# Edge terms of four graphs: one product on a block-diagonal operand, or four short products on row groups

## The chip, the cores and the metric

The kernel runs on one core of a Trainium2 chip. The metric is the time of the program on the device, in microseconds, as the median of several runs. All data are fp32.

## The reference, cut to what matters

There are 128 graphs of 128 nodes with 256 channels each. The program is two graph layers, one after the other. The change lies in the first, in the branch that weighs messages by the distance of node features. With `h` the normalised input after a relu:

```
s    = h @ w_se.T + b_se                                  # 3 numbers for each node
sq   = sum(s * s, -1)
dist = sq[:, :, None] + sq[:, None, :] - 2 * s @ s.T      # for each graph, 128 x 128
A    = exp(-dist) * adj
msg  = relu(h @ w_msg.T + b_msg)
x_nmp = A @ msg                                           # for each graph
```

`x_nmp`, together with the output of a convolution branch (`x_conv`) and `h`, goes into a gated unit (three gates, 768 by 512 and 768 by 256 weights). The second layer runs five small graph convolutions on the first 25 nodes of each graph.

The exponent can be had from one matrix product with five rows for each graph. The left operand has the rows `2 s` (three), `-1` and `-sq`; the right one `s` (three), `sq` and `1`. Their product is `2 s s' - sq' - sq`, which is `-dist`.

## The kernel before

**Blocks.** Four graphs make a block (`BB` = 4), so there are 32 blocks. The program has a front part (normalisation, and the convolution through spectra), and then a loop over the 32 blocks that computes gates and, beside them, everything else that is left. Instructions of each engine run in a fixed order. In the loop that order is made by a scheduler of the framework from the program's order and from when it expects buffers and inputs to be ready; the front part has an order written by hand.

**The loop.** `gates(i, step, nxt)` computes the gated unit of block `i`. Its products (L599) are a Strassen scheme: 7 products of quarters for each gate part, each of up to three input pairs. After each of the 7 outputs, `between()` (here `step`) advances a generator by one step: either `beside_gates(i + 1)`, which makes the next block's inputs, or a piece of the second layer. `beside_gates` runs, in this order and spread over the steps, `messages` (L505 to L518), `conv_out` (L487 to L494), `edge_terms` (L525 to L529), `edges` (L538 to L541), `x_nmp` (L551 to L556) and the pieces of `back`, the end of block `i - 1`.

**Edge terms.** `messages` leaves the five-row operands in `lr`, in which the nodes stand on the partitions and each graph has a stretch of 32 columns, five of them filled (three sums, and the constants of L447 and L448). `edge_terms` transposes both halves of `lr` on TensorE (L525), so that graph `b` has its five rows on the partitions 32b to 32b+4. The left half is copied to `lt` by ScalarE (L527). The right half is copied by VectorE to `rt` (L529), four times side by side, and each copy is multiplied by a mask `bm`, which keeps only the 32 partitions of its own graph: `rt` is block-diagonal, 128 rows by 512 columns. `bm` is made once by GpSimd (L471 to L474). `edges` then needs one product of all 128 rows by 512 columns (L538) into one PSUM bank, one exponential over 512 columns on ScalarE (L540) and one product with the adjacency mask `at` on VectorE (L541). `x_nmp` takes the result `e` as the moving operand of eight products (L551).

**Banks.** All TensorE outputs are tiles of one pool with eight buffers, `bank()`, each one PSUM bank of 512 columns. A product that is given a bank waits until its last user has emptied it.

**Row groups.** One other place in the kernel has products on groups of 32 rows. `weight_spectra` (L162) keeps 17 taps on the partitions 32r to 32r+16 and issues four products in a row, for r from 0 to 3, each to a bank of its own.

**Names that the prediction uses.** `xc` (L494) is the convolution branch's output, made on ScalarE from `u` (L493, VectorE). `m` (L602, L610) is a gate output copied out of PSUM by ScalarE; `u` of L607, L612 and L617 and the outputs of L604, L614 and L620 are sums of gate outputs on VectorE and GpSimd. L633 works on the reset gate on VectorE. `ab` (L775, L780) and `hn` (L765, L766) are in `back`, and `xa` is where `ab` is stored by the queue of SyncE (SP). L575 makes operands of the Strassen scheme. `nt` and `dck` are small loads of the second layer.

Of the kernel before, what the change touches and what calls it, by code (L numbers as in the profile page):

```python
# [8 lines left out]
F32 = mybir.dt.float32  # L9
AF = mybir.ActivationFunctionType  # L10
ALU = mybir.AluOpType
AX = mybir.AxisListType

P = 128
# [3 lines left out]
BB = 4  # L18
# [56 lines left out]
def gnn_kernel(ctx: ExitStack, tc: tile.TileContext, io, out0: bass.AP, out1: bass.AP):  # L75
    nc = tc.nc
    x, adjT = io["x"], io["adjT"]
    B, N, D = x.shape
# [7 lines left out]
    cst = ctx.enter_context(tc.tile_pool(name="cst", bufs=1))  # L86
# [5 lines left out]
    def bank():  # L92
        return psum.tile([P, 512], F32, tag="bank", name="bank")
# [327 lines left out]
    wk = ctx.enter_context(tc.tile_pool(name="wk", bufs=1, reuse_waits="tile"))  # L421
# [5 lines left out]
    def load(i):  # L427
# [9 lines left out]
        for b in range(BB):  # L437
# [28 lines left out]
    nc.vector.tensor_mul(nb2, vec[:, V_B2:V_B2 + 5 * C].rearrange("p (g c) -> p g c", c=C),  # L466
                         nw[:, :, None].to_broadcast([P, 5, C]))


    bm = cst.tile([P, BB], F32)  # L470
    nc.gpsimd.memset(bm, 1.0)  # L471
    nc.gpsimd.affine_select(out=bm, in_=bm, compare_op=ALU.is_ge, fill=0.0, base=0,
                            pattern=[[-32, BB]], channel_multiplier=1)
    nc.gpsimd.affine_select(out=bm, in_=bm, compare_op=ALU.is_ge, fill=0.0, base=31,  # L474
                            pattern=[[32, BB]], channel_multiplier=-1)

    A_s, xcs, xns, ts, msgs, outs, lrs, xts = ({} for _ in range(8))

    def conv_out(i):
# [41 lines left out]
    def edge_terms(i):  # L521

        ps = bank()
        for k in range(2):
            nc.tensor.transpose(ps[:, k * P:(k + 1) * P], lr[:, k].rearrange("p b r -> p (b r)"), ident)  # L525
        lt = wk.tile([P, P], F32, tag="lt", name="lt", bufs=2)
        nc.scalar.copy(lt, ps[:, :P])  # L527
        rt = wk.tile([P, BB, N], F32, tag="rt", name="rt", bufs=1)
        nc.vector.tensor_tensor(rt, ps[:, None, P:2 * P].to_broadcast([P, BB, N]),  # L529
                                bm[:, :, None].to_broadcast([P, BB, N]), op=ALU.mult)  # L530
        lrs[i] = lt, rt

    def edges(i):

        at, _, _ = loaded.pop(i)
        lt, rt = lrs.pop(i)
        pd = bank()
        nc.tensor.matmul(pd, lt, rt.rearrange("p b n -> p (b n)"), start=True, stop=True)  # L538
        e = wk.tile([P, BB, N], F32, tag="e", name="e", bufs=1)
        nc.scalar.activation(e.rearrange("p b n -> p (b n)"), pd, AF.Exp)  # L540
        nc.vector.tensor_mul(e, e, at)  # L541
        A_s[i] = e

    def x_nmp(i):
# [391 lines left out]
    def beside_gates(i):  # L936

        ends = back(i - 2, *back_loads(i - 2)) if i > 1 else iter(())
        if i < NBLK:
            parts = messages(i)  # L940
            next(parts)
            yield
            next(parts)
            next(ends, None)
            yield
            inverse = conv_out(i)
            next(inverse)
            next(ends, None)
            yield
            edge_terms(i)  # L950
            next(ends, None)
            yield
            for _ in inverse:
                yield
            edges(i)
            yield
            next(ends, None)
            yield
            yield
            yield from x_nmp(i)  # L960
        for _ in ends:
            yield
            if i == NBLK:
                yield
# [174 lines left out]
```

## Time and profile before

| | |
|---|---|
| three runs | 1934.36, 1942.66, 1935.14 us; median 1935.14 |
| profiled execution, its own time | 1944.77 us |
| its span, first to last instruction | 1943.0 us |
| granted TensorE clock, mean | 0.992 of full speed |
| TensorE busy (matmuls) | 1901.1 us |
| VectorE, ScalarE, GpSimd busy | 1296.3, 713.2, 609.2 us |
| L538, both passes of 32 products | 64 records |
| moved from and to HBM | 178.66 and 85.14 MB |

How to read it: the profile is of one execution, whose own time is longer than the median of the three runs. PE is TensorE's matmuls, PEld its weight loads, DVE VectorE, ACT ScalarE, POOL GpSimd, SP SyncE, which only issues transfers here. An fp32 product appears as two records, one for each pass, so counts of matmuls are twice those of the program. The length of a matmul's record includes the way through the pipeline, and its end is modelled; what a matmul costs in a dense row is the distance to the start of the next. In the lines of groups, `out<-in` are the program's names, then come shapes, the count, and after the bar busy time, mean ns of one, and the idle time of the engine before them.

### The profile page before, as it was taken

Reading aid. Unit: us, or ns where it says so; the run is one execution under the profiler, and the core shown is the slowest. Engines: PE = TensorE matmul, PEld = TensorE weight load, DVE = VectorE, ACT = ScalarE, POOL = GpSimd, SP = SyncE. Lnnn points to the kernel's source line nnn. Section 1 sums busy time; section 2 is a strip of 40 time slices with the busy share of each in tenths; the row PEclk is TensorE's granted clock in tenths of the full one; section 3 lists DMA queues with packets and bytes.
Section 4 is the critical chain, followed back from the end, with each engine's and each line's share of the span. In section 5 each row is a group of like instructions: output and inputs, shape, how many; then the busy total and the mean of one; then the engine's idle time right before and its main releaser. Section 6 shows DMA issues by size and latency. Waiting matters only on the chain.

```text
span 1943.0 us, 29921 instructions
## 1 busy us (share of the span) xinstructions
PE 1901.1 (98%) x10418; PEld 1652.7 (85%) x10418; DVE 1296.3 (67%) x3247; ACT 713.2 (37%) x1459; POOL 609.2 (31%) x681
## 2 busy tenths in 40 slices
PE   8999898999899999999999999999999999999999
PEld 7888787988788888888888888888878888888887
DVE  5676457754587777777756577787756587777643
ACT  4553113421143334334333434334334434333334
POOL 1012442135233433443322243343322143343300
PEclk9999999999899999999999999999999999999999
DMA  8787975459843223233323533224333523222125
GB/s 309 293 315 226 323 260 194 142 181 309 267 135 98 72 72 102 68 81 110 81 84 92 142 81 100 70 71 116 86 82 87 147 75 105 74 72 64 44 88 154
DMA packets 248853, 265.76 MB, mean 137 GB/s; under 512 B 106850, under 2 KB 223927, under 8 KB 244223
## 3 DMA queue, kind: packets, MB, share of 16 engines
q1 hardware_dynamic: 236767, 196.74, 35.8%
q10 hardware_dynamic: 11936, 67.11, 8.9%
q8 instruction: 83, 1.36, 0.3%
q14 instruction: 67, 0.55, 0.1%
HBM read 178.66 MB, written 85.14 MB: 136 GB/s over the span
## 4 chain that ended last, share of the span: by engine, by line
PE 90%; DMA 6%; DVE 2%; issue 1%; ACT 1%; POOL 0%; SPq 0%; ACTq 0%; POOLq 0%; DVEq 0%
PE bank L599 44%; PE bank L314 6%; PE bank L505 5%; PE bank L919 5%; PE bank L859 5%; PE bank L223 5%; PE bank L487 3%; PE bank L551 3%; PE bank L238 3%; DMA v<-vd 3%; PE bank L309 3%; PE bank L490 1%; PE bank L162 1%; PE bank L538 1%; PE bank L838 1%; PE bank L770 1%
## 5 line engine op out<-in xcount | busy, mean ns | idle before, releaser
L599 PE MATMUL bank<-t,sw 128*128 128x256 f32 x1152 | 290.9, 379 | 0.2 <-POOL t L573 0.2
L612 POOL TENSOR_TENSOR u<-u,m 128x256 f32<-128x256 f32 x128 | 92.9, 726 | 594.4 <-ACT m L610 532.2
L599 PEld LDWEIGHTS bank<-t,sw 128*128 128x128 f32 x1152 | 215.3, 190 | 30.1 <-issue 2.3
L599 PE MATMUL bank<-t,wih 128*128 128x256 f32 x768 | 197.2, 379 | 0.0
L599 PEld LDWEIGHTS bank<-t,wih 128*128 128x128 f32 x768 | 143.4, 190 | 19.3 <-DVE u L617 0.5
L306 POOL TENSOR_TENSOR vs<-v 128x512 f32<-128x512 f32 x78 | 100.5, 1307 | 138.7 <-DMA v<-vd 74.9
L223 PE MATMUL bank<-wc,ht 128*128 128x256 f32 x512 | 125.1, 399 | 6.1 <-ACT ht L210 6.1
L505 PE MATMUL bank<-wms,ht 128*128 128x259 f32 x512 | 122.3, 381 | 0.0
L223 PEld LDWEIGHTS bank<-wc,ht 128*128 128x128 f32 x512 | 100.4, 201 | 22.6 <-ACT ht L210 8.4
L599 PE MATMUL bank<-t,whh 128*128 128x256 f32 x384 | 114.6, 380 | 0.3 <-DVE z L614 0.3
L599 PE MATMUL bank<-xc,wih 128*128 128x256 f32 x384 | 114.7, 380 | 0.0
L599 PE MATMUL bank<-xn,wih 128*128 128x256 f32 x384 | 114.6, 380 | 0.0
L919 PE MATMUL bank<-w,hh 128*125 128x256 f32 (+9 forms) x480 | 113.5, 380 | 0.3 <-DVE hh L864 0.3
L599 PE MATMUL bank<-ht,whh 128*128 128x256 f32 x384 | 110.3, 381 | 0.0
L505 PEld LDWEIGHTS bank<-wms,ht 128*128 128x128 f32 x512 | 97.3, 190 | 14.7
L304 DVE SCALAR_TENSOR_TENSOR s<-X 128x256 f32<-128x256 f32 x78 | 48.0, 618 | 90.4 <-PE bank L314 90.1
L859 PE MATMUL bank<-ax,w 128*128 128x500 f32 (+8 forms) x416 | 107.0, 396 | 0.0
L617 DVE TENSOR_TENSOR u<-bank,u 128x256 f32<-128x256 f32 x128 | 53.7, 420 | 74.0 <-PE bank L599 74.0
L919 PEld LDWEIGHTS bank<-w,hh 128*125 128x125 f32 (+9 forms) x480 | 84.3, 177 | 18.6 <-issue 0.9
L509 ACT ACTIVATE msg<-msg 128x512 f32<-128x512 f32 x64 | 40.3, 630 | 162.0 <-DVE msg L506 160.2
L193 POOL TENSOR_TENSOR rs<-ve,mhalf 128x4 f32<-128x4 f32 x32 | 32.3, 1010 | 211.7 <-DVE ve L191 211.7
L311 ACT COPY k<-bank 128x256 f32<-128x256 f32 x78 | 29.0, 373 | 179.4 <-PE bank L309 70.2
(191 smaller groups left out, 4305.3 us busy)
## 6 DMA issues: line engine op xcount, KB each, us to landing
v<-vd SPq DMA_DIRECT2D x80, 512.0 KB
vd<-sp ACTq DMA_DIRECT2D x8, 2560.0 KB
yd<-ys ACTq DMA_DIRECT2D x40, 512.0 KB
w<-in_w_dram SPq DMA_DIRECT2D x40, 512.0 KB
htd<-ht ACTq DMA_DIRECT2D x32, 512.0 KB
ht<-htd SPq DMA_DIRECT2D x32, 512.0 KB
ym<-yd SPq DMA_DIRECT2D x32, 512.0 KB
xt<-in_xT_dram SPq DMA_DIRECT2D x32, 512.0 KB
```

What stands on the lines that cost most here:

```text
L223: nc.tensor.matmul(pv[:, bb, :], ht[:, c, b * N:(b + 1) * N], wc1[:, c, :], start=c == 0, stop=c == C - 1)
L238: nc.tensor.matmul(ps[:, bb * 2 * LW:(bb + 1) * 2 * LW], h1[:, 2 * h + bb, c * P:(c + 1) * P], fd, start=True, stop=True)
L306: nc.gpsimd.tensor_tensor(vs, vr, vi, op=ALU.add)
L309: nc.tensor.matmul(p1[:, :D], a[:, c], vs[:, c], start=c == 0, stop=c == C - 1)
L314: nc.tensor.matmul(ps[:, k * D:(k + 1) * D], u[:, c], w[:, c], start=c == 0, stop=c == C - 1)
L487: nc.tensor.matmul(ps[:, b * N:(b + 1) * N], ym[:, b, o * P:(o + 1) * P], idm, start=b == 0, stop=False)
L505: nc.tensor.matmul(ps[:, :D + 3], ht[:, c, b * N:(b + 1) * N], wms[:, c, :], start=c == 0, stop=c == C - 1)
L551: nc.tensor.matmul(ps[:, b * N:(b + 1) * N], msg[:, b, c * P:(c + 1) * P], e[:, b, :], start=True, stop=True)
L599: nc.tensor.matmul(ps, w, d, start=n == 0, stop=n == len(pairs) - 1)
L612: nc.gpsimd.tensor_tensor(got["u4"], got["u2"], got["m5"], op=ALU.add)
L859: nc.tensor.matmul(pv[:, q - q0, :], w1s[k5 + g][:, c, q * P:(q + 1) * P], xv[:, c], start=c == 0, stop=c == C - 1)
L919: nc.tensor.matmul(ps[:n1, :D], hh[:, q, at:at + n1], w2s[k5 + g][:, q, :], start=q == 0, stop=q == HID // P - 1)
```

## The change

`rt` and the mask `bm` go. `lt` now takes both halves of the transposed operands, in one copy on ScalarE. The one product of 128 rows by 512 columns becomes four of 5 rows by 128 columns, each on the partitions of its own graph and each into a bank of its own. The exponential becomes four, one for each bank, and the product with the adjacency mask two, each behind two exponentials. What is computed stays the same.

```diff
-    bm = cst.tile([P, BB], F32)
-    nc.gpsimd.memset(bm, 1.0)
-    nc.gpsimd.affine_select(out=bm, in_=bm, compare_op=ALU.is_ge, fill=0.0, base=0,
-                            pattern=[[-32, BB]], channel_multiplier=1)
-    nc.gpsimd.affine_select(out=bm, in_=bm, compare_op=ALU.is_ge, fill=0.0, base=31,
-                            pattern=[[32, BB]], channel_multiplier=-1)
...
         for k in range(2):
             nc.tensor.transpose(ps[:, k * P:(k + 1) * P], lr[:, k].rearrange("p b r -> p (b r)"), ident)
-        lt = wk.tile([P, P], F32, tag="lt", name="lt", bufs=2)
-        nc.scalar.copy(lt, ps[:, :P])
-        rt = wk.tile([P, BB, N], F32, tag="rt", name="rt", bufs=1)
-        nc.vector.tensor_tensor(rt, ps[:, None, P:2 * P].to_broadcast([P, BB, N]),
-                                bm[:, :, None].to_broadcast([P, BB, N]), op=ALU.mult)
-        lrs[i] = lt, rt
+        lt = wk.tile([P, 2, P], F32, tag="lt", name="lt", bufs=2)
+        nc.scalar.copy(lt.rearrange("p k n -> p (k n)"), ps[:, :2 * P])
+        lrs[i] = lt

     def edges(i):

         at, _, _ = loaded.pop(i)
-        lt, rt = lrs.pop(i)
-        pd = bank()
-        nc.tensor.matmul(pd, lt, rt.rearrange("p b n -> p (b n)"), start=True, stop=True)
+        lt = lrs.pop(i)
+        pd = [bank() for _ in range(BB)]
+        for b in range(BB):
+            g = slice(32 * b, 32 * b + 5)
+            nc.tensor.matmul(pd[b][:, :N], lt[g, 0, :], lt[g, 1, :], start=True, stop=True)
         e = wk.tile([P, BB, N], F32, tag="e", name="e", bufs=1)
-        nc.scalar.activation(e.rearrange("p b n -> p (b n)"), pd, AF.Exp)
-        nc.vector.tensor_mul(e, e, at)
+        for b in range(BB):
+            nc.scalar.activation(e[:, b, :], pd[b][:, :N], AF.Exp)
+            if b % 2:
+                nc.vector.tensor_mul(e[:, b - 1:b + 1, :], e[:, b - 1:b + 1, :], at[:, b - 1:b + 1, :])
         A_s[i] = e
```

## The prediction

> **What bounds the kernel now.** The page comes first: its line of busy time by engine, its slices, and the shares of the chain that ended last.
>
> ```profile
> PE 1901.1 (98%) x10418; PEld 1652.7 (85%) x10418; DVE 1296.3 (67%) x3247; ACT 713.2 (37%) x1459; POOL 609.2 (31%) x681
> ...
> PE   8999898999899999999999999999999999999999
> ...
> PE 90%; DMA 6%; DVE 2%; issue 1%; ACT 1%; POOL 0%; SPq 0%; ACTq 0%; POOLq 0%; DVEq 0%
> ```
>
> TensorE is busy in nearly every slice and makes up 90% of the chain. A busy share can still hide stalls, so the next view is one block of four graphs in the gate stage, 591.90 to 629.05 us, in the table of busy time by stretch (the columns after the stretch: length, then PE, PEld, DVE, ACT and POOL busy, granted clock, DMA share, GB/s).
>
> ```profile
> 591.90:629.05 37.15, 37.15 (x190) 32.79 (x189) 27.84 (x66) 13.98 (x24) 14.74 (x17) 1.00 0.31 83
> ```
>
> All 37.15 us are TensorE's, at full clock, and the next block (629.05 to 666.20) again takes 37.15. VectorE has 9.3 us free, ScalarE 23. Last, the timeline of TensorE around the product in question (start, length, instruction):
>
> ```profile
> 619.05 0.59 PE L599 MATMUL bank<-t,sw 128*128 128x256 f32 x2
> 619.48 0.59 PE L599 MATMUL bank<-t,whh 128*128 128x256 f32 x2
> 619.91 1.02 PE L538 MATMUL bank<-rt,lt 128*128 128x512 f32 x2
> 620.77 0.59 PE L599 MATMUL bank<-ht,sw 128*128 128x256 f32 x2
> ...
> 622.79 0.59 PE L599 MATMUL bank<-xc,wih 128*128 128x256 f32 x2
> ...
> 625.38 1.05 PE L551 MATMUL bank<-e,msg 128*128 128x128 f32 x8
> ```
>
> An fp32 product is two records (x2), one pass each. The lengths include the pipeline, so the cost of a product is the distance to the next start: 0.43 us for 256 columns, and 620.77 - 619.91 = 0.86 us for L538's 512, without a hole before or after. From about 590 to 1860 us I find no distance between two starts longer than the columns explain by more than 0.1 us. So time that L538 gives back shortens the program, as long as nothing that TensorE then asks for is late.
>
> **What the Trainium skill says.**
> - "TensorE: Matmul & The Clock Gate", Part 3 (packing small matmuls): products on different groups of 32 rows run at once, some 4 ns apart. The trace agrees: L162, which reads 17 rows at partition 32r, shows four starts about 7 ns apart.
> - "TensorEngine Tiling (Array Packing)", Key Properties: a change of tiling mode drains TensorE. The trace agrees and gives the price below, some 0.27 us for a visit.
> - "PSUM — Partial Sum Buffer", PSUM bank collisions: different row tiles may not use one bank at the same time; there are eight banks. Hence four banks here in place of one, as L162 does it too.
> - "ScalarE: Activation LUTs", What ACT_TABLE_LOAD costs: an activation with immediate scale and bias takes 186 ns + 0.833 ns per element, and neighbours overlap by 93 ns. For 512 that is 613 ns; the trace has 598.
>
> **The change on TensorE.** The nearest thing in the trace is L162's visit between two full-array stretches:
>
> ```profile
> 90.20 0.59 PE L223 MATMUL bank<-wc,ht 128*128 128x256 f32 x2
> 90.73 1.13 PE L162 MATMUL bank<-gt,w 17*128 17x80 f32 x32
> 91.79 0.33 PE L209 MATMUL bank<-ident,ln 128*128 128x128 f32 x1
> ```
>
> The last L223 pass starts at 90.42. From there to L209 is 1.37 us. L223's own pass takes 0.216. The 32 records come as eight fours, 0.112 apart (90.900, 91.012, 91.124 ...), 0.89 in all. What remains, 1.37 - 0.216 - 0.89 = 0.265, is the switch: 0.093 going in, 0.061 at the second four, the rest going out.
>
> The change needs four products of 128 columns, eight records, so two fours: 2 x 0.112 = 0.224, plus 0.265, is 0.489 in place of 0.857, a gain of 0.368. Two things may take from it. In the changed order of instructions the bank for the fourth product has a semaphore instruction of its own in 26 of the 30 later blocks. At 101.96 us one between L162's fours shifts the last by 0.05, and that visit is longer by 0.05. I count it: gain 0.318. And the passes have 128 columns, L162's 80. The distance of 0.112 also holds for dense 128-column passes (L487), so it stays; but the drain may start 48 columns later, 0.04 us. I count nothing for it and keep 0.278 as the lower end. Upper end 0.368.
>
> Sum: 26 x 0.318 + 4 x 0.368 = 9.7 us (8.4 to 11.0) for blocks 2 to 31.
>
> Blocks 0 and 1 are not dense. In block 0, TensorE waits 2.0 us for e, behind xc on ScalarE (until 520.10). Exp and mask product then take 0.60 + 1.26 in a row. Cut in parts they overlap, and the first two L551 products may begin after the first half: some 0.5 us sooner. But loads and degree work (waits on nt and dck in the chain until 565 us) may absorb it, and their order on VectorE and SP shifts there. I take 0.5, from -0.5 to 1.5.
>
> Total 10.2 us: 0.53%.
>
> **The change on the other engines.**
>
> ```profile
> L529 DVE TENSOR_TENSOR rt<-bank,bm 128x512 f32<-128x512 f32 x32 | 21.6, 675 | 0.0
> L541 DVE TENSOR_TENSOR e<-e,at 128x512 f32<-128x512 f32 x32 | 23.4, 730 | 1.6 <-ACT e L540 1.6
> L540 ACT ACTIVATE e<-bank 128x512 f32<-128x512 f32 x32 | 19.1, 598 | 0.5 <-PE bank L538 0.2
> L527 ACT COPY lt<-bank 128x128 f32<-128x128 f32 x32 | 8.5, 266 | 45.0 <-PE bank L525 44.9
> ```
>
> VectorE loses rt (0.675 a block) and gets two half products for one; a half is 0.36 (half of L541) to 0.65 (L575, beside POOL), I take 0.42: +0.11. Net it is relieved by 0.57 a block; worth nothing in time, since TensorE is the bound. ScalarE: lt grows to 256 columns, 0.36 by L602, so +0.10. One exp becomes four of 128; by the page's price 0.293 + 3 x 0.200 = 0.89, so +0.29. Unhidden neighbours would give 4 x 0.27 (L527's copy) = 1.08. Both lie in ScalarE's free time. POOL loses bm's three instructions, once, early: nothing. SP: the load of the next mask moves ahead of the five stores of xa, and waits there for the second mask product. That product ends before ab, which the stores wait for, so nothing queued behind it is late.
>
> **Who waits for that.** ScalarE and VectorE around the block:
>
> ```profile
> 621.03 1.28 ACT L540 ACT_TABLE_LOAD   x1
> 622.33 0.60 ACT L540 ACTIVATE e<-bank 128x512 f32<-128x512 f32 x1
> ```
> ```profile
> 621.85 0.43 DVE L614 TENSOR_TENSOR nh<-bank,u 128x256 f32<-128x256 f32 x1 [1.52 <-POOL u L612]
> ```
>
> Start of exp is set by the table load behind m of L610, which the change doesn't touch. Exps end at 622.33 + 0.89 = 623.22; the mask halves follow L633 (623.27) and end near 624.1. L551 asks for e at 625.38 - 0.32 = 625.06: 0.95 us to spare. Behind the halves on VectorE stand ab, nh (L620) and nn (L604), some 0.4 later than now; their banks are asked for 2 us and more after that.
>
> The four banks are held from 619.98 until the exps end. Meanwhile the next four outputs take the other four banks. The fifth, xc,wih (622.79 now, 622.47 then), is the tightest: in the changed order it takes the bank of ht,sw, which L614 empties at 621.85 + 0.43 = 622.28: 0.19 us to spare, less the semaphore's delay. A gain over some 0.45 a block would turn into a wait there; 0.318 does not. If exps were 0.3 longer, nothing changes: the first exp's bank is asked for only at 624.2.
>
> **Rivals.**
> 1. *The main case*, 0.77: fours overlap as L162's do, 1923 to 1928.
> 2. *More*, 0.09: the semaphore and part of the switch hide behind the long queue, or block 0 gives over 1 us: 1920 to 1923. For: semaphore instructions between the dense L599 passes cost nothing; against: between L162's fours they do, and all of its regular visits pay the switch.
> 3. *The gain is held up*, 0.09: a bank or e comes late once TensorE runs ahead (L614 above, or new order around blocks 0 and 1). If half is lost, 1930; if all, 1935. Against: the spare times above.
> 4. *Slower*, 0.05: the four products don't overlap. L162's groups stand in a queue of 32; here are eight passes, with waits between them for four different banks. One after another they need 8 x 0.112 = 0.896, plus 0.265 and 0.05: 1.21 in place of 0.857, 30 x 0.354 = 10.6 us slower, 1945.8. It decides as soon as the eight passes take over 0.857 - 0.315 = 0.54 us, an overlap below 1.65 in place of 4. Against: all four banks are free when TensorE comes to them at 619.9 (the last to be emptied by hn, L765, at 619.03).
> That the change doesn't do what it says would be rival 4: single records at 0.11 us distance.
>
> **How the numbers follow.** The durations come from the profiled execution: span 1943.0, its time 1944.77, 9.6 us above the median of 1935.14. The sum is a difference, so it is taken from the median: 1935.14 - 10.2 = 1924.9. Range: 1920.5 to 1931, which leaves out rival 4, most of full hold-up and little else. A change of under 0.5% (9.7 us) is about what a measurement of this kernel can't tell from none. The main case lies across that line: 0.46 of its 0.77 are beyond it. Faster: 0.46 + 0.09 = 0.55. Within: 0.31 + 0.09 = 0.40. Slower: 0.05.
>
> **What would show it.** Right: the new matmuls in fours some 7 ns apart, two fours 0.17 apart; from the L599 pass before them to the one after some 0.75 (now 1.07); a dense block of 36.83 us in place of 37.15; no new wait of TensorE on exp or e. Wrong: passes at 0.11 one by one (rival 4), a hole ahead of xc,wih or L551 (rival 3), or a visit of 0.83, where the longer drain is real and the sum is 8.4.

## The result, and the profile after

| | before | after |
|---|---|---|
| median (lowest to highest) of 14 runs each | 1939.41 us (1932.32 to 1944.15) | 1932.47 us (1925.84 to 1939.46) |
| ratio of after to before | | 0.9969, 95% interval 0.9955 to 0.9983 |
| profiled execution, its own time; its span | 1944.77; 1943.0 us | 1931.98; 1930.2 us |
| one dense block, visit to visit | 37.15 us | 36.925 us |

By the ratio the change makes the kernel faster by 0.31%, or 6.0 us (3.3 to 8.7); the two medians differ by 6.9. The direction is as forecast. The size is not: 10.2 us were forecast, and 1932.47 lies above the range of 1920.5 to 1931.0. In the traces blocks 2 to 31 fall 3.4 us short of the forecast, by the step that priced the visit, and blocks 0 and 1 another 2.0; that is more than the 4.2 us that are missing, but within the interval. The median of before is itself 4.3 us higher over 14 runs than over the three that the forecast stood on.

In the changed kernel `edges` has L529 (products), L532 (exponentials) and L534 (mask products), `edge_terms` L517 and L519, the gate products are L592, `x_nmp` is L544; these were L538, L540, L541, L525, L527, L599 and L551. The page, busy time and shares of the chain:

```profile
PE 1888.0 (98%) x10610; PEld 1644.3 (85%) x10610; DVE 1307.9 (68%) x3247; ACT 721.6 (37%) x1556; POOL 611.2 (32%) x678
...
PE 91%; DMA 5%; DVE 2%; POOL 1%; issue 1%; ACT 1%; SPq 0%; ACTq 0%; DVEq 0%; POOLq 0%
```

TensorE is still what everything waits for. VectorE did not get lighter, but not through the instructions that were changed: two mask halves take 1.28 us a block where `rt` and the whole mask product took 1.40. What grew is the scaling of `ae` by `dinv`, which the change does not touch, first before, then after:

```profile
L753 DVE TENSOR_SCALAR ae<-ae,dinv 100x24 f32<-100x24 f32 (+3 forms) x160 | 28.5, 247 | 0.2
```
```profile
L746 DVE TENSOR_SCALAR ae<-ae,dinv 100x24 f32<-100x24 f32 (+3 forms) x160 | 41.9, 328 | 1.1
```

Why it takes longer no run shows. One dense block in the table of busy time by stretch (length, then PE, PEld, DVE, ACT, POOL, granted clock, DMA share, GB/s):

```profile
649.27:686.20 36.93, 36.93 (x196) 32.64 (x195) 28.48 (x66) 14.19 (x27) 14.73 (x17) 1.00 0.32 79
```

All 36.93 us are TensorE's at full clock, as before. A block is 0.226 shorter where 0.318 was forecast. TensorE's timeline around one visit:

```profile
611.82 0.59 PE L592 MATMUL bank<-t,whh 128*128 128x256 f32 x2
612.35 0.50 PE L529 MATMUL bank<-lt 5*128 5x128 f32 x8
612.78 0.70 PE L592 MATMUL bank<-ht,sw 128*128 128x256 f32 x2
613.32 0.59 PE L592 MATMUL bank<-t,sw 128*128 128x256 f32 x2
...
614.90 0.59 PE L592 MATMUL bank<-xc,wih 128*128 128x256 f32 x2
...
617.49 1.05 PE L544 MATMUL bank<-e,msg 128*128 128x128 f32 x8
```

Look at the third line. Two gate passes take 0.59 everywhere else; here 0.70, and the next product starts 0.54 later (613.32 - 612.78) instead of 0.43. So the price of the visit (TensorE's turn from the gate products to the edge products and back) is not fully paid when the first pass after it starts: something of 0.104 us is still in that pass. Neither xc,wih nor L544 has a hole before it.

What that something is, TensorE's timeline of weight loads shows, first of before:

```profile
619.27 0.41 PEld L599 LDWEIGHTS bank<-t,whh 128*128 128x128 f32 x2
619.70 0.41 PEld L538 LDWEIGHTS bank<-rt,lt 128*128 128x128 f32 x2
620.34 0.19 PEld L599 LDWEIGHTS bank<-ht,sw 128*128 128x128 f32 x1 [0.24 <-issue]
```

and of after:

```profile
611.61 0.41 PEld L592 LDWEIGHTS bank<-t,whh 128*128 128x128 f32 x2
612.35 0.31 PEld L529 LDWEIGHTS bank<-lt 5*128 5x128 f32 x8 [0.33 <-issue]
612.78 0.30 PEld L592 LDWEIGHTS bank<-ht,sw 128*128 128x128 f32 x2
```

Before, the weights of L538 are loaded from 619.70, while the pass ahead of it still runs; its own first pass starts at 619.91. After, no load is ahead of its product. L529's first loads start at 612.35 together with its first products, and those of the gate product after the visit at 612.78 together with that product. Both loads lie open, that is, they are not hidden beside the pass ahead: once going in and once coming out. That the extra time in these passes is the load is read from where the loads start and from the sizes below. No run put other weights behind the visit.

### The profile page after: what moved, and what is told of

Its sections match the earlier page's. It is cut to its first block, busy times and chain, and to the rows that moved or that the text cites. A ratio compares the mean times of both kernels' runs of the same rounds, so it can differ in the third digit from the quotient of the medians.

```text
span 1930.2 us, 30443 instructions
## 1 busy us (share of the span) xinstructions
PE 1888.0 (98%) x10610; PEld 1644.3 (85%) x10610; DVE 1307.9 (68%) x3247; ACT 721.6 (37%) x1556; POOL 611.2 (32%) x678
## 4 chain that ended last, share of the span: by engine, by line
PE 91%; DMA 5%; DVE 2%; POOL 1%; issue 1%; ACT 1%; SPq 0%; ACTq 0%; DVEq 0%; POOLq 0%
PE bank L592 44%; PE bank L314 6%; PE bank L497 5%; PE bank L912 5%; PE bank L852 5%; PE bank L223 5%; PE bank L309 3%; PE bank L238 3%; PE bank L544 3%; PE bank L479 3%; PE bank L162 2%; DMA v<-vd 2%; PE bank L482 1%; PE bank L831 1%; PE bank L763 1%; PE bank L209 1%
## 5 line engine op out<-in xcount | busy, mean ns | idle before, releaser
L592 PE MATMUL bank<-t,sw 128*128 128x256 f32 x1152 | 291.5, 380 | 1.0 <-POOL t L566 1.0
L592 PEld LDWEIGHTS bank<-t,sw 128*128 128x128 f32 x1152 | 215.5, 190 | 31.3 <-issue 2.3
L592 PE MATMUL bank<-t,wih 128*128 128x256 f32 x768 | 197.2, 379 | 0.0
L592 PEld LDWEIGHTS bank<-t,wih 128*128 128x128 f32 x768 | 143.4, 190 | 19.3 <-DVE u L610 0.5
L592 PE MATMUL bank<-t,whh 128*128 128x256 f32 x384 | 114.9, 381 | 0.0
L592 PE MATMUL bank<-xc,wih 128*128 128x256 f32 x384 | 114.4, 379 | 0.4 <-DVE nh L607 0.4
L592 PE MATMUL bank<-xn,wih 128*128 128x256 f32 x384 | 114.3, 379 | 0.0
L592 PE MATMUL bank<-ht,whh 128*128 128x256 f32 x384 | 109.8, 379 | 0.0
L632 ACT ACTIVATE nn<-nn,vec 128x512 f32<-128x512 f32 x64 | 46.2, 722 | 134.6 <-DVE nn L631 134.6
```

What stands on the lines that cost most here:

```text
L592: nc.tensor.matmul(ps, w, d, start=n == 0, stop=n == len(pairs) - 1)
```

## The experiments

The reading is one number that these traces give to 0.01 us: the distance from one block's visit to the next in the dense stretches. Next to it stands the price of a visit: from the start of the last gate pass ahead of it to the start of the second gate pass behind it, less two ordinary passes (0.432). The ratio is to the kernel before, run beside it.

| kernel | price of a visit, us | block, us | ratio (95%) |
|---|---|---|---|
| before | 1.290 - 0.432 = 0.858 | 37.151 | |
| after | 1.062 - 0.432 = 0.630 | 36.925 | 0.9969 (0.9955 to 0.9983) |
| full4 | 1.326 - 0.432 = 0.894 | 37.187 | 1.0023 (1.0009 to 1.0037) |
| twice | 1.285 - 0.432 = 0.853 | 37.147 | 1.0003 (0.9989 to 1.0017) |
| halves | 1.262 - 0.432 = 0.830 | 37.122 | 1.0001 (0.9982 to 1.0021) |
| twovisits | 2 x (1.050 - 0.432) = 1.236 | 37.527 | 1.0056 (1.0036 to 1.0076) |
| bf16_block | 0.648 - 0.432 = 0.216 | 36.507 | 0.9929 (0.9911 to 0.9947) |
| fours_bf16 | 0.796 - 0.432 = 0.364 | 36.657 | 0.9922 (0.9900 to 0.9944) |
| early | as after from block 2 on | 36.925 | 0.9959 (0.9946 to 0.9972) |
| ae_gpsimd | as after | 36.925 | 0.9933 (0.9908 to 0.9958) |
| bf16_early | as bf16_block from block 2 on | 36.507 | 0.9897 (0.9865 to 0.9928) |

In every row the difference of the block from before's is the difference of the visit's price, to 0.003 us. So in dense blocks nothing but the visit changes TensorE's time.

The theory (A below): a visit on row groups costs a fixed sum of about 0.40 us, and then 0.112 for each four of passes, four records that start almost together. The fixed sum is a gap of 0.093 behind the last full-array pass, an open weight load of 0.107 in the first four (the second four starts 0.213 after the first, not 0.107), a gap of 0.093 behind the last four, and an open load of 0.104 in the pass after it. The rivals put the shortfall down to the four banks and their semaphores (B), or let the cost grow with the number of short products (C).

**full4**: four products without row groups.

```diff
+        rt = ...                                  # and bm, as in the kernel before
-            g = slice(32 * b, 32 * b + 5)
-            nc.tensor.matmul(pd[b][:, :N], lt[g, 0, :], lt[g, 1, :], start=True, stop=True)
+            nc.tensor.matmul(pd[b][:, :N], lt, rt[:, b, :], start=True, stop=True)
```

> Four products of all 128 rows by 128 columns on the block-diagonal operand of the kernel before, into four banks, with the changed kernel's four exponentials and two mask products. Nothing of the row groups is left. Theory A (the gain and its short-fall both come from the switch to row groups and back: about 0.40 us a visit): no switch here, so the visit costs 8 passes x 0.112 = 0.896 in place of 0.857, the pass after it takes the usual 0.216, and the dense block is 37.15 + 0.04 = 37.19 us; the time is that of the kernel before within 2 us. Rival B (the missing 0.09 us a block is due to the four banks, their semaphores or the order of exponentials): the pass after the visit is late here too, by 0.1, and the block is 37.28 us or more.

TensorE's timeline at this visit:

```profile
615.42 1.05 PE L539 MATMUL bank<-rt,lt 128*128 128x128 f32 x8
616.31 0.60 PE L602 MATMUL bank<-ht,sw 128*128 128x256 f32 x2
```

The pass behind the visit takes 0.219, and the pair 0.60, not 0.70. The block is 37.187, as theory A has it, so four banks, four exponentials and the halved mask product cost TensorE nothing in a dense block. The time was a miss: 4.5 us slower (1.7 to 7.2), where 2 at most were expected. The blocks give 1.1 of it. Two things may give the rest, and no run parts them. In its profile blocks 0 and 1 take 77.0 us against 75.0 and 72.5 in two profiles of before; TensorE waits 5.6 us for `dinv` there, on which more below. And its 20 runs had a mean granted clock of 0.9918, the 54 of before beside them 0.9937. Among those 54 the time falls by 2.3 us for each 0.001 of clock (correlation -0.86), so the clock alone would go with some 4 us.

**twice**: the same visit with twice the passes.

```diff
-        for b in range(BB):
-            g = slice(32 * b, 32 * b + 5)
-            nc.tensor.matmul(...)
+        for _ in range(2):
+            for b in range(BB):
+                g = slice(32 * b, 32 * b + 5)
+                nc.tensor.matmul(...)
```

> The changed kernel with each of its four products issued twice in a row of eight (the second writes over the first with the same values). Theory A (a visit costs some 0.40 us fixed, going in and coming out, and 0.112 for each four of passes after that): 2 more fours, 0.22 us, so a block of 36.93 + 0.22 = 37.15 us, and the time of the kernel before within 2 us. Rival C (the cost goes with the number of short products, each four at about a quarter of the whole 0.742 - 0.216 = 0.526 visit, 0.26): 0.53 more, a block of 37.45 us, some 9 us slower than the kernel before.

Eight passes more cost 0.223 (0.853 - 0.630), the block is 37.147, and the pair behind the visit has the same 0.70 in its timeline. Rival C falls: inside a visit a four costs 0.112, and the rest is paid once.

**twovisits**: the four products in two visits of two.

```diff
-        pd = [bank() for _ in range(BB)]
-        for b in range(BB):
+        for h in range(0, BB, 2):
+            pd = [bank() for _ in range(2)]
+            for b in range(h, h + 2):
...
+            yield
```

> The changed kernel with its four products in two visits of two each, a stretch of full-array gate products between them. Theory A (cost by visit): the second visit costs another 0.40 us of switch plus its own two passes of 0.107, less one four saved in neither: a visit of two products has as many steps as one of four, so a block of 36.93 + 0.40 + 0.22 = 37.55 us, some 12 us slower than the kernel before (0.6%). Rival C (cost by product, not by visit): half the products in each, the sum unchanged, a block of about 36.95 us and a gain like the changed kernel's.

A block is 37.527 us, 0.602 more than after, and the program is 0.56% slower than before. A visit of two graphs costs 0.618, practically what a visit of four does (0.630).

**halves**: two products on 64 rows.

```diff
-            g = slice(32 * b, 32 * b + 5)
-            nc.tensor.matmul(pd[b][:, :N], lt[g, 0, :], lt[g, 1, :], start=True, stop=True)
+            g = slice(64 * k, 64 * k + 64)
+            nc.tensor.matmul(pd[k][:, :2 * N], lt[g], rt[g, 2 * k:2 * k + 2, :]..., start=True, stop=True)
```

> Two products of 64 rows by 256 columns on halves of the block-diagonal operand, into two banks, with two exponentials of 256 and two mask products. Theory A (switch 0.40 us, then the passes: two row halves side by side, 2 passes of 256 columns at 0.214): 0.40 + 0.43 = 0.83 us in place of 0.857, so a block of 37.12 us, no measurable gain; if the switch is dearer for wider weight loads, up to 37.2. Rival D (the switch of the blind prediction, 0.265): 0.69 us, a block of 36.99 us.

37.122, as theory A had it, and no measurable gain: this shape takes half of the passes' time away (two of 0.214 instead of two of 0.429), and the switch takes it back. Gap in, gap out and both open loads have the sizes they had with 32 rows.

**bf16_block and fours_bf16**: is the switch worth paying at all? Both split s and sq into a high and a low bf16 part, which needs 16 rows for each graph and one pass in place of two. The first has before's block-diagonal product, the second after's row groups. The split adds small VectorE operations to `messages`; what it does to the accuracy is not treated here.

```diff
+        hi = wk.tile([P, BB, 4], BF16, tag="hi", name="hi", bufs=2)
+        nc.vector.tensor_copy(hi, lr[:, 1, :, 0:4])
+        nc.vector.tensor_tensor(lr[:, 1, :, 4:8], lr[:, 1, :, 0:4], hi, op=ALU.subtract)
...
-        lt = wk.tile([P, P], F32, tag="lt", name="lt", bufs=2)
+        lt = wk.tile([P, P], BF16, tag="lt", name="lt", bufs=2)
...
-        rt = wk.tile([P, BB, N], F32, tag="rt", name="rt", bufs=1)
+        rt = wk.tile([P, BB, N], BF16, tag="rt", name="rt", bufs=1)
```

> The kernel before with its one block-diagonal product of 128 rows by 512 columns, but with s and sq split into a high and a low bf16 part (16 rows for each graph in place of 5), so that it needs one pass in place of two and no switch. Theory A (time is TensorE's distance alone): 0.857 becomes 512 columns in one pass at full-array rate, 0.2155 to 0.22 us, so a block of 37.15 - 0.64 = 36.51 us and 30 x 0.64 = 19 us less than the kernel before (1.0%), some 13 us less than the changed kernel. Rival E (four more small VectorE operations, some 0.17 us each, or the bank of xc,wih come too late for a TensorE that runs 0.64 us ahead): part of it turns into a wait of TensorE inside the block, a block of 36.6 to 36.9 us.

> The changed kernel's four products on row groups with the same split into bf16 parts: 16 rows, one pass each, so one four in place of two. Theory A (the switch has the same price whatever the passes are): gap 0.093 in, exposed weight load 0.107, one pass 0.107 with 0.02 for the four, gap 0.093 out, the next product's exposed load 0.104, in all 0.52 in place of the kernel before's 0.857: a block of 36.82 us, 10 us faster than the kernel before, and 0.3 us a block slower than the block-diagonal product in bf16. Rival F (the exposed load going in is a price of fp32 weights): that load shrinks to half or less and the block is 36.76 us or below.

The visit of bf16_block:

```profile
616.91 0.38 PE L548 MATMUL bank<-rt,lt 128*128 128x512 bf16 x1
617.13 0.59 PE L609 MATMUL bank<-ht,sw 128*128 128x256 f32 x2
```

and of fours_bf16, products and then their weight loads:

```profile
609.85 0.23 PE L541 MATMUL bank<-lt 16*128 16x128 bf16 x4
610.01 0.70 PE L604 MATMUL bank<-ht,sw 128*128 128x256 f32 x2
```
```profile
609.85 0.10 PEld L541 LDWEIGHTS <-lt 16*128 16x128 bf16 x4 [0.33 <-issue]
```

bf16_block is as expected: one product of 0.216 instead of 0.858, a block of 36.507, 0.71% faster than before (0.53 to 0.89). Rival E falls; the added VectorE work is hidden. fours_bf16 is a miss of theory A, which had 36.82; rival F had 36.76 or below, and 36.657 was measured. Two things were priced wrongly. A bf16 pass of 128 columns is not 0.107: bf16_block passes 512 in 0.216, so 128 would take 0.054. And from the first four to the next gate product there are only 0.164 us, of which 0.054 is that pass and 0.01 the four's stagger; some 0.10 is left for open load and gap together, where fp32 has 0.20. One load's record has 0.091 us against 0.181 in fp32. So load and gap together are about halved with the operand's type (how the 0.10 divides between them the trace does not say), and the pass behind the visit, an fp32 one, still pays its 0.104.

The two programs' times do not differ measurably, though fours_bf16's blocks are longer by 0.15: the intervals overlap, and the front part and blocks 0 and 1 of their profiles differ by more than 30 blocks of 0.15.

**Second profiles** of before, after and bf16_block show which parts of a program's time belong to it. The run `bf16_gpsimd` is the kernel of bf16_block, unchanged.

> The kernel before, a second profile. If block periods are the same to 0.01 us from one execution to the next and the front part and blocks 0 and 1 are not, the block is 37.15 us again, while the front part ends within some 8 us and blocks 0 and 1 within some 1.5 us of the first profile.

> The changed kernel, a second profile: blocks of 36.925 us again if the period is a property of the program; blocks 0 and 1 tell whether their 0.6 us over the kernel before is real (theory: the order of VectorE around the degree chain costs it, so it is there again) or varies with when the loads land (rival: it moves by 1 us or more).

> The block-diagonal product in bf16 parts once more, unchanged, as a second profile: the block is 36.51 us again; the front part ends within 2 us of the first profile's 503.5 us if its length belongs to the program, and anywhere from 497 to 507 us if it varies from one execution to the next.

| profile | end of L314 (front part) | from there to block 2's visit | block 2's to block 31's visit | rest |
|---|---|---|---|---|
| before | 507.0 | 75.0 | 1214.6 | 146.5 |
| before, second | 506.6 | 72.5 | 1214.6 | 147.6 |
| after | 498.8 | 75.6 | 1208.3 | 147.5 |
| after, second | 500.6 | 74.8 | 1208.3 | 147.4 |
| bf16_block | 503.5 | 76.9 | 1195.2 | 147.3 |
| bf16_block, second | 499.9 | 75.4 | 1195.6 | 147.1 |

The stretch from block 2 to block 31, 29 distances between visits, repeats to 0.4 us. The front part, in which the change takes out only the three short GpSimd instructions of `bm`, does not: 3.6 us between two profiles of one program. That is why the profiled execution of after is 12.8 us shorter than that of before although the medians differ by 7: 8 us of it are front part. By the means of the two profiles each, blocks 2 to 31 give 6.3 us, blocks 0 and 1 take 1.5 and the rest 0.4: together a gain of 4.4, inside the interval of 3.3 to 8.7. Whether the change also shortens the front part is not shown: over all 14 profiles it ended at 499.9 to 507.0 us with `bm` in the program and at 497.8 to 504.5 without. Blocks 0 and 1 of before differ by 2.4 us between its two profiles, more than the 1.5 expected. In the first of them the granted clock in the stretch from 500 to 576 us was 0.93, in the second 0.98. Those of after differ by 0.8, both at 0.95.

**early and ae_gpsimd**: blocks 0 and 1. TensorE's waits from 500 to 576 us (in total, times, longest), first before, then after:

```profile
PE bank L551 <- DVE e L541: 2.0, 1, 2.0
PE bank L709 <- DVE dinv L704: 0.8, 1, 0.8
```
```profile
PE bank L702 <- DVE dinv L697: 5.4, 1, 5.4
...
PE bank L544 <- DVE e L534: 1.0, 1, 1.0
```

The wait for `e` is 1.0 us shorter: exponentials and mask products in parts do overlap, by more than the forecast's 0.5. But a wait of 5.4 us for `dinv` has come, where 0.8 was. `dinv` (L704, now L697) is the end of the degree chain on VectorE, which first sums three loaded tiles, `dga`, `dgb` and `dgc`. VectorE's timeline in before, with the start of the chain's next step in the last line:

```profile
526.39 1.71 DVE L688 TENSOR_REDUCE dinv<-dgb 128x60 f32<-128x1500 f32 x1
...
532.27 1.27 DVE L686 TENSOR_REDUCE dinv<-dgc 100x16 f32<-100x400 f32 x5
...
534.25 0.29 DVE L692 TENSOR_SCALAR dinv<-dinv 128x273 f32<-128x273 f32 x1
```

and in after:

```profile
519.03 1.28 DVE L679 TENSOR_REDUCE dinv<-dgc 100x16 f32<-100x400 f32 x5 [1.84 <-DMA dgc<-in_adjB_dram]
...
521.13 1.28 DVE L679 TENSOR_REDUCE dinv<-dgc 100x16 f32<-100x400 f32 x5 [0.50 <-DMA dgc<-in_adjB_dram]
...
523.12 1.71 DVE L681 TENSOR_REDUCE dinv<-dgb 128x60 f32<-128x1500 f32 x1
...
525.30 0.29 DVE L685 TENSOR_SCALAR dinv<-dinv 128x273 f32<-128x273 f32 x1
```

The order of the two sums has turned round. Before, VectorE summed `dgb` first and then did not wait for `dgc`; now it stands 2.3 us for `dgc`, and sums `dgb` after that. Measured from the transposes of block 1's `lr` (539.70 before, 525.73 after), the chain's next step came 5.45 us ahead of them before and comes 0.43 ahead now. That is most of the 5.4 us for which TensorE now stands. But the wait is more than the loss, since TensorE also comes to its place sooner. From the end of L314 to these transposes it took 32.7 us in before, at a granted clock of 0.84, and 27.0 in after, at 1.00. The first product with `dinv` starts 36.9 and 34.2 us after the end of L314 in the two profiles of before, 35.8 and 36.2 us in those of after: 1.5 to 2 us later than in before's second profile, in which the clock up to the transposes was 0.94, and not later than in its first. Further on, the sum of `ae` (L743) also waits 0.9 us for its load ahead of the chain's reciprocal.

In the next run `edge_terms0` and `edges0` are the functions of the kernel before.

```diff
-            edge_terms(i)
+            (edge_terms0 if i < 2 else edge_terms)(i)
...
-            edges(i)
+            (edges0 if i < 2 else edges)(i)
```

> The changed kernel with blocks 0 and 1 made as in the kernel before (block-diagonal product, one exponential, one mask product); blocks 2 to 31 as changed. This puts VectorE's and TensorE's order around the degree chain back. Theory G (the changed order there costs blocks 0 and 1 some 1 to 2 us: TensorE waits 5.4 us for dinv in place of 0.8): the wait for dinv is below 1.5 us again, from the end of L314 to block 2's visit it takes 72.5 to 75.0 us as in the two profiles of the kernel before, blocks still 36.925 us, and the time is 1 to 2 us below the changed kernel's. Rival H (those blocks are set by the loads of their inputs, whatever the order): 74.8 to 75.6 us as in the changed kernel, with the waits elsewhere.

```diff
-        nc.vector.tensor_add(ae[:n4], ae[:n4], ie[:n4])
+        nc.gpsimd.tensor_add(ae[:n4], ae[:n4], ie[:n4])
```

> The changed kernel with one edit: the sum of ae and the diagonal (L743) is made by GpSimd, so that VectorE's degree chain stands behind no load of ae. Theory G1 (that load is what holds dinv up, 0.9 us of it, and the rest of the 5.4 us is the chain's own length on VectorE behind TensorE's moved transposes): the wait for dinv shrinks by 0.9 to 1.3 us only, to some 4.2 us. Rival G2 (the ae sum is the whole cause): the wait falls below 1.5 us. Blocks stay at 36.925 us unless GpSimd, waiting for ae, holds back an operand of the gates.

TensorE's waits in early, for the same stretch:

```profile
PE bank L732 <- DVE dinv L727: 0.8, 1, 0.8
```

The wait for `dinv` is before's again (that for `e`, 2.0, too), `dgb` is summed ahead of `dgc` again, and from the end of L314 to block 2's visit it takes 72.6 us, 2.6 less than the mean of the two profiles of after (75.2). Theory G holds for the wait. Part of the 2.6 us may be the granted clock, 0.98 in this stretch in early and 0.95 in both profiles of after; but fours_bf16, with the turned order, took 75.3 at 0.98. In the time the gain cannot be seen: 1932.72 us against 1932.47, with ratios of overlapping intervals; in its profile the front part was longer in turn (506.5). ae_gpsimd moves the wait for `dinv` only to 5.1 us, less than G1 had, and blocks 0 and 1 took 76.5; so the sum of `ae` is not the cause. G1's other half does not hold as it was put: TensorE's transposes have not moved among their neighbours. They come sooner in time, and VectorE's chain, which stands for `dgc`, has not come sooner with them: its next step is 26.5 us after the end of L314 in after, 24.6 in early. In this kernel, too, `dgc` is summed first, as in every run that changes the edge products of blocks 0 and 1, full4 and halves among them; so it is not the row groups that turn the order. That the time of ae_gpsimd nevertheless came out at 0.67% below before, lower than after's, nothing in its trace explains.

**bf16_early** puts together what the runs pointed to.

> The block-diagonal product in bf16 parts for blocks 2 to 31, and blocks 0 and 1 in fp32 and in the order of the kernel before. Theory: the two gains add. The wait for dinv is 0.8 us, from the end of L314 to block 2's visit it takes 72.5 to 75.0 us in place of 75.4 to 76.9, blocks take 36.51 us, and the time is 1 to 3 us below that of the bf16 product in all blocks (1924.07 us, measured beside a kernel before at 1939.66), some 18 us below the kernel before. Rival: the front part ends at 506.1 to 506.7 us as in all three profiles with the old order in blocks 0 and 1, against 499.9 and 503.5 us in the two profiles of the bf16 product in all blocks: then what blocks 0 and 1 give is taken back ahead of them, and the time is the same or up to 3 us longer.

In the trace both gains are there: the wait for `dinv` is 0.8, from the end of L314 to block 2's visit it takes 73.5 us, and blocks are 36.507. The program is 1.03% faster than before (0.72 to 1.35), 1921.39 us beside 1938.82. The rival did not happen in this profile, where the front part ended at 502.1 (506.5 to 507.0 in the three profiles with the old order, by the end of the last record). It is the fastest by ratio of all that were run, but its interval overlaps those of bf16_block and fours_bf16, so that the two gains add in the time is not shown.

## Why the prediction was wrong

By its own steps:

- **What bounds the kernel: right.** What a visit gives or takes shows in the block, to 0.003 us.
- **The fours overlap: right.** Starts lie 7 ns apart, and twice puts a four at 0.112. Rival 4 did not happen; full4, without overlap, measures what it would have been without a switch: 0.894.
- **The price of the switch: this step failed.** It put a visit at 0.489 + 0.05 = 0.539; measured is 0.630. The term that was mis-sized is "the rest out". It was read from L162's visit up to the start of the first L209 pass and stopped one record too early. In that same trace the second L209 pass starts at 91.957, which is 0.166 behind the first, where all later ones are 0.109 apart, and the record that the forecast itself showed is 0.33 long where the next is 0.27. There lay 0.057 of open load, in sight. With the weights of a gate product it is 0.104, so the visit that served as the model shows only half of what was missing. The switch was taken for a drain alone. The Trainium skill, "TensorE: Matmul & The Clock Gate", LDWEIGHTS (loading the stationary operand), prices a load by its columns, P / 1.2 ns: 107 for 128 columns. Both open loads measure that, 0.107 and 0.104 us; L209's, with 0.057, does not. A price near the measured one was to be had and was not in the sum.
- **The lower end, + 0.04 for wider passes: real, but at another place than was put, and counted as nothing.** From the last record of the visit to the next pass it is 0.201 us with L162's 80 columns and 0.200 with 128; it is the second four that comes at 0.213 instead of 0.173, since it stands behind an open load and a whole pass.
- **The semaphore instruction, 0.05 in 26 blocks: its cost is not there.** L529 has 56 such instructions, but of blocks 2 to 31 only block 2's visit is stretched (0.866 in place of 0.742, from the start of the last gate pass ahead to that of the first behind). The sum over the three terms: 0.539 + 0.104 + 0.04 - 0.05 = 0.633.
- **Blocks 2 to 31**: 9.7 us forecast; 6.3 measured from block 2's visit to block 31's. Each of these distances is 0.226 shorter but the one behind block 2's visit, which is 37.94 us where it was 37.92.
- **Blocks 0 and 1: wrong sign.** Half of the argument was right (1.0 us less waiting for `e`). What was named as a danger, the shifted order, is there: over two profiles each, with the same mean granted clock of 0.95, the way from the front part's end to block 2's visit is 1.5 us longer in place of 0.5 shorter, and early, in which the old order is back, has the old wait.
- **The other engines: hidden, as said, though not all of the sizes fit.** The groups of after:

```profile
L534 DVE TENSOR_TENSOR e<-e,at 128x256 f32<-128x256 f32 x64 | 38.5, 639 | 2.6 <-ACT e L532 2.4
...
L532 ACT ACTIVATE e<-bank 128x128 f32<-128x128 f32 x128 | 25.2, 283 | 0.8 <-PE bank L529 0.4
```

  `lt` takes 0.371 (0.36 forecast), in L519's group. Four exponentials take 0.79 in a dense block, less than the forecast's 0.89. A mask half is 0.639 in the mean, at the upper end of 0.36 to 0.65 and not 0.42, so VectorE is relieved by 0.13 us a block and not by 0.57. That a dense block has 28.48 us of VectorE in place of 27.84 comes from L746, whose five instructions take 1.42 us of the block; with the sum ahead of them `ae` takes 1.79 in place of 1.22. L544 still finds `e` ready: the second mask half ends at 616.80 and L544 starts at 617.49. Rival 3 did not happen in the dense blocks.
- **The base.** The forecast took 10.2 us from a median of three runs. The ratio that it implies, 0.9947, also lies outside the interval, so the base alone is not the reason.

## What to carry to other kernels

Read the price of a switch up to the second record behind it, and compare both records' lengths with their neighbours': a pass can start on time and still carry its weight load. Row groups pay once for a visit, here 0.40 us in fp32, so gather as many short products as there are into one visit, or ask first whether fewer passes on the whole array cost less: one bf16 pass on the block-diagonal operand took 0.216 where the best row-group visit took 0.364. And where a scheduler makes the order, an edit can turn round two instructions elsewhere (the sums of `dgb` and `dgc`; the wait for `dinv` went from 0.8 to 5.4 us, and blocks 0 and 1 took about 1.5 us longer); the places where the program is not dense need their own look.

## What was not expected of the hardware

- Across a switch between full array and row groups no weights were loaded ahead, in either direction, in any kernel with row groups: the pass behind the visit took 0.320 instead of 0.216, to 0.001 us the same whether the visit had 4, 8 or 16 records, 32 or 64 rows, fp32 or bf16.
- Load and gap go with the operand's type: 0.181 and 0.091 us for a load's record, and some 0.20 and 0.10 for load and gap together. The Trainium skill, "TensorE: Matmul & The Clock Gate", Weight-path perf modes — Fast Weight Load (FWL) and DoubleRow, has a load twice as fast for 128 weights that are not fp32; the records agree. For the gap no page and no run gives the reason.
- The front part's end varies by 3.6 us between two profiles of one program, which is more than half of what the change gave. Over all 14 profiles it ended later, as a rule, where the granted clock up to 500 us was lower (0.976 to 0.990, correlation -0.83), but not by the clock alone: at 0.983 it was 507.0 in before and 499.9 in twovisits. What sets either stays open.
